# Four two-bank PSUM tiles split into one-bank tiles, and half of a transposition moved, in a graph attention kernel

## The chip, the cores and the metric

The kernel runs on one core of one Trainium2 chip. The metric is the device time of one execution in microseconds (us). All data are 32-bit floats.

## What is computed

The input x has 16 batches of 1024 nodes with 256 channels; `adj` is one 1024 x 1024 matrix shared by all batches. Two residual layers follow each other, each with a layer norm over the channels. The reference, cut to what matters:

```
# layer 0: x = layernorm(x + attention(x))
c_adj = mean over channels of x                       # one number a node
A     = 2 * | |sigmoid(c_adj[m] - c_adj[n]) - 0.5| - 0.5 |   # symmetrised
g     = relu((x^T @ (adj * A)) * para)                # 256 x 1024 a batch
q     = g^T, in 4 heads of 64
k, v  = split(x @ kv_w), in 4 heads of 64
out   = softmax(q k^T * scale) v

# layer 1: x = layernorm(x + 0.5 * (x + h))
h = relu(x @ w1_loop + adj @ (x @ w1_neigh) + b1)     # 128 channels
h = relu(h @ w2_loop + adj @ (h @ w2_neigh) + b2)     # 256 channels
```

In the second graph convolution the kernel multiplies `adj @ h` first (the product u) and applies `w2_neigh` after it.

## The kernel before

**Layout.** 1024 nodes are 8 tiles of 128 partitions (NT), 256 channels are 2 (NC), and a row of 1024 is 2 halves of 512 (NJ, FB), the size of one bank of PSUM. [...]The pool `psum` gives them out in two rings: `big_psum` has three tiles of two banks each, `bank_psum` has two tiles of one bank each. A new tile takes the place of the oldest of its ring, and the first instruction that writes it waits until the last reader of the old one is done.

**Order.** Instructions of each engine run in the order in which the code issues them (`manual_schedule`); there is no planner. One pass of the loop over b does the attention of batch b, the graph convolution of batch b - 1, and the preparation of batch b + 1. The attention has four units (a pair of heads and half of the queries each). For each unit:

- `scores(u)`: eight tiles s of scores on TensorE in the big ring (L377), eight exponentials on ScalarE (L380), and on VectorE the running sum of the eight results, acc (L384, L386), its transposition accB (L388) and its reduction den_part (L390). Ahead of the fourth tile, `halfway` puts in `add` of the unit before (den_ps in the bank ring, L409, read on VectorE by L413 to L415, then L417 to L420), and in unit 1 also `means` of the next batch (L206 in the bank ring, read by L213).
- `outputs(u)`: sixteen products with v, in the tile av of the bank ring (L397). VectorE transposes av into o (L401) after all of its work of `scores(u)`.
- Between the units stand the pieces of the graph convolution: `first` after unit 0, `second` after unit 1, `last` after unit 2. In the last batch only `first` stands there, and `second` and `last` come after the squares of the norm.

After unit 3 come the product g of the next batch (`step`, L345, with its weights wg from L331, L332 and L337), the blocked norm (`mean`, `squares`, `variance`, with two more tiles of the bank ring for its sums), and `keys` and `values` of the next batch. After the loop, `first`, `second` and `last` run once more for batch 15.

**Where the change is.** `values` makes v in two big tiles of four pieces of 256 columns each, and ScalarE empties a big tile in two copies. `first` makes t1 (L489, L492), then one big tile for h: the loop products of both halves (L497), then the products with the transposed adjacency for each half (L502), each half emptied by a ReLU into h1T (L504). `second` transposes h1T in one big tile (L514, L515), and makes u in another (L520, L522). `last` uses uT and h1T (L531, L532) and is read by VectorE (L534, L537). SBUF rows such as pr, acc, accB, t1, h1T, h1, uT and the loaded xB tiles share one ring of 15 (`row_tile`). SyncE's queue issues the DMAs: x and xB of the next batch, the spreading of the normed rows into x1, and the output.

Of the kernel before, what the change touches and what calls it, by code (L numbers as in the profile page):

```python
# [12 lines left out]
AF = mybir.ActivationFunctionType  # L13
# [5 lines left out]
def kernel(  # L19
# [31 lines left out]
    nc = tc.nc  # L51

    B, N, C = x.shape
    P = 128
    NT = N // P
# [4 lines left out]
    FB = 512  # L60
    NJ = N // FB
    TJ = FB // P
# [18 lines left out]
    def big_psum(name):  # L81
        return psum.tile([P, N], F32, tag="big", name=name, bufs=3)

    def bank_psum(name):
        return psum.tile([P, FB], F32, tag="bank", name=name, bufs=2)
# [6 lines left out]
    def row_tile(name):  # L92
        return work.tile([P, N], F32, tag="row", name=name, bufs=ROWS)

    def load_blocked(b, name):
        tiles = []
        for cc in range(NC):
            t = row_tile(f"xB_{name}_{cc}")
            for a in range(Q):
                c0 = cc * P + a * S  # L100
                nc.sync.dma_start(
                    out=t[a * S:(a + 1) * S, :].rearrange("k (bn r) -> k bn r", r=S),
                    in_=x[b, :, c0:c0 + S].rearrange("(bn k) r -> k bn r", k=S))
            tiles.append(t)
        return tiles
# [7 lines left out]
    w1l_sb = const.tile([P, NC, HID], F32, name="w1l_sb")  # L113
# [3 lines left out]
    b1_sb = const.tile([HID, 1], F32, name="b1_sb")  # L117
# [18 lines left out]
    ident = const.tile([P, P], F32, name="ident")  # L136
# [18 lines left out]
    adjT_sb = const.tile([P, NT, N], F32, name="adjT_sb")  # L155
# [38 lines left out]
    def prepare(blocked, name):  # L194

        xT = channel_major(blocked, f"xT_{name}")
        part = small.tile([P, NC, NB], F32, tag="part", name=f"part_{name}", bufs=2)
        for cc in range(NC):
            nc.vector.tensor_reduce(part[:, cc, :], blocked[cc].rearrange("p (bn r) -> p bn r", r=S), AX.X, ALU.add)
        return xT, part  # L200
# [90 lines left out]
    def keys(b, xT):  # L291
        kT = work.tile([P, NC, N], F32, tag="kT", name=f"kT_{b}")
        for kb in range(NC):
            pk = big_psum(f"k_ps_{b}_{kb}")
            for j in range(NJ):
                for cc in range(NC):
                    nc.tensor.matmul(pk[:, ts(j, FB)], kvw_sb[:, cc, ts(kb, P)], xT[:, cc, ts(j, FB)],  # L297
                                     start=(cc == 0), stop=(cc == NC - 1))
            nc.scalar.copy(kT[:, kb, :], pk)
        return kT  # L300

    def values(b, xT):
        v = work.tile([P, NT, C], F32, tag="v", name=f"v_{b}")
        per = N // C
        for g in range(NT // per):
            pv = big_psum(f"v_ps_{b}_{g}")
            for i in range(per):
                for cc in range(NC):
                    nc.tensor.matmul(pv[:, ts(i, C)], xT[:, cc, ts(g * per + i, P)], kvw_sb[:, cc, C:2 * C],  # L309
                                     start=(cc == 0), stop=(cc == NC - 1))  # L310
                if i % 2:
                    nc.scalar.copy(v[:, g * per + i - 1:g * per + i + 1, :],  # L312
                                   pv[:, (i - 1) * C:(i + 1) * C].rearrange("p (i c) -> p i c", c=C))
        return v

    class Queries:
# [161 lines left out]
    class GraphConv:  # L478
# [5 lines left out]
        def first(self):  # L484
            b, xT = self.b, self.xT
            p1 = big_psum(f"t1_ps_{b}")
            for t in range(NT):
                for cc in range(NC):
                    nc.tensor.matmul(p1[:, ts(t, HID)], xT[:, cc, ts(t, P)], w1n_sb[:, cc, :],  # L489
                                     start=(cc == 0), stop=(cc == NC - 1))  # L490
            t1 = row_tile(f"t1_{b}").rearrange("p (t f) -> p t f", f=HID)
            nc.scalar.copy(t1, p1.rearrange("p (t f) -> p t f", f=HID))  # L492

            ph = big_psum(f"h1_ps_{b}")
            for j in range(NJ):
                for cc in range(NC):
                    nc.tensor.matmul(ph[:, ts(j, FB)], w1l_sb[:, cc, :], xT[:, cc, ts(j, FB)],  # L497
                                     start=(cc == 0), stop=False)
            self.h1T = row_tile(f"h1T_{b}")
            for j in range(NJ):  # L500
                for mt in range(NT):
                    nc.tensor.matmul(ph[:, ts(j, FB)], t1[:, mt, :], adjT_sb[:, mt, ts(j, FB)],  # L502
                                     start=False, stop=(mt == NT - 1))
                nc.scalar.activation(self.h1T[:, ts(j, FB)], ph[:, ts(j, FB)], AF.Relu, bias=b1_sb)  # L504

        def second(self):

            b = self.b
            h1 = row_tile(f"h1_{b}")
            pt = big_psum(f"h1n_ps_{b}")  # L510
            for j in range(NJ):
                for i in range(TJ):
                    t = j * TJ + i
                    nc.tensor.transpose(pt[:, ts(t, P)], self.h1T[:, ts(t, P)], ident)  # L514
                nc.scalar.copy(h1[:, ts(j, FB)], pt[:, ts(j, FB)])  # L515
            pu = big_psum(f"u_ps_{b}")
            self.uT = row_tile(f"uT_{b}")
            for j in range(NJ):
                for mt in range(NT):
                    nc.tensor.matmul(pu[:, ts(j, FB)], h1[:, ts(mt, P)], adjT_sb[:, mt, ts(j, FB)],  # L520
                                     start=(mt == 0), stop=(mt == NT - 1))
                nc.scalar.copy(self.uT[:, ts(j, FB)], pu[:, ts(j, FB)])  # L522

        def last(self):
            b, x = self.b, self.x
# [22 lines left out]
    def run():  # L548
# [13 lines left out]
        for t in range(3):  # L562
            q.weigh(t)
        v = values(0, xT)
        for t in range(NT):
            if t + 3 < NT:
# [4 lines left out]
        for b in range(B):  # L571
# [20 lines left out]
            def halfway(u):  # L592
                att.add(u - 1)
                if u == 1 and more:
                    ready["mean"] = means(ready["part"], str(b + 1))

            between = [first, second, last] if more else [first]
            for u in range(len(UNITS)):
                if b == 0:
# [13 lines left out]
            if more:  # L613
# [26 lines left out]
                norm.scale()  # L640
                norm.spread()
                kT, v = keys(b + 1, xT), values(b + 1, xT)
            else:
                att.add(3)
                norm.mean()
                norm.squares()
                second()
                norm.variance()
                norm.scale()
# [28 lines left out]
    with tc.If(count < P):  # L678
        with tc.For_i(0, B, 1) as b:
            xb = load_x(b, "z")  # L680
            xT, part = prepare(load_blocked(b, "z"), "z")
            q = Queries("z", xb, *means(part, "z"))
            kT, v = keys("z", xT), values("z", xT)
            for t in range(NT):
                q.weigh(t)
                q.step(t)
            safe_attention("z", xb, q.end(), kT, v)
            layernorm(xb, "za")
            conv = GraphConv("z", xb, channel_major(blocked_of(xb, "z"), "x1T_z"))
            conv.first()  # L690
            conv.second()
            conv.last()
            conv.moments()
            conv.finish(out[b])
# [29 lines left out]
```

## Time and profile before

| | us |
|---|---|
| median of three runs | 2475.52 (2475.50 to 2475.76) |
| the profiled execution | 2474.71 |
| its span, first to last instruction | 2473.0 |
| mean granted TensorE clock | 0.99 of full speed |

| engine | busy us | share of the span |
|---|---|---|
| TensorE matmuls (PE) | 2343.9 | 95% |
| TensorE weight loads (PEld) | 1093.1 | 44% |
| VectorE (DVE) | 1540.1 | 62% |
| ScalarE (ACT) | 970.0 | 39% |
| GpSimd (POOL) | 128.6 | 5% |

A busy share is an average over stages that differ. A TensorE row shows an instruction from its start to the end of its latency, so rows of the same engine overlap and a busy time is not the time in which the engine could do no more. One matmul of the code is two instructions in the profile. Brackets behind a row give the idle time of the engine ahead of it and the instruction that ended it. The batches in the middle of the run are alike to a hundredth of a microsecond and follow each other every 150.15 us, so one of them stands for them all.

### The profile page before, as it was taken

How to read it: one execution, taken by the hardware profiler on the slowest of the kernel's cores; microseconds unless marked ns; L12 is line 12 of the kernel's file. 1: busy time of each engine (PE TensorE's matmuls, PEld its weight loads, DVE VectorE, ACT ScalarE, POOL GpSimd, SP SyncE). 2: the span in 40 equal slices, each digit the busy share in tenths (PEclk: the TensorE clock that was granted, in tenths of full speed). 3: DMA queues.
4: the chain of work that ended last, by engine and by line, in shares of the span. 5: the costliest groups of instructions: out<-in, count | busy, mean ns of one | idle time of the engine just before them, and what ended most of it. 6: DMA issues, size and time to landing. Idle time of an engine off the chain costs nothing.

```text
span 2473.0 us, 22370 instructions
## 1 busy us (share of the span) xinstructions
PE 2343.9 (95%) x8534; PEld 1093.1 (44%) x8534; DVE 1540.1 (62%) x2015; ACT 970.0 (39%) x1044; POOL 128.6 (5%) x45
## 2 busy tenths in 40 slices
PE   7899999999999999999999999999999999999976
PEld 4344444444444344444444444444443444444443
DVE  2865846748476484755758467484764847557553
ACT  3533524425343343524435244253433435244410
POOL 0000000100001010010100001000010100101000
PEclk9999999999999999999999999999999999999988
DMA  7422050320503113050230503205031140502001
GB/s 172 67 29 42 1 85 1 46 40 1 85 1 54 32 25 61 0 85 1 40 46 1 85 1 46 40 1 86 1 57 29 27 59 0 86 1 40 12 5 48
DMA packets 466674, 95.01 MB, mean 38 GB/s; under 512 B 431360, under 2 KB 465024, under 8 KB 466560
## 3 DMA queue, kind: packets, MB, share of 16 engines
q1 hardware_dynamic: 464864, 87.74, 23.2%
q10 hardware_dynamic: 1696, 5.77, 0.6%
q8 instruction: 69, 1.13, 0.2%
q14 instruction: 45, 0.37, 0.1%
HBM read 59.90 MB, written 16.78 MB: 31 GB/s over the span
## 4 chain that ended last, share of the span: by engine, by line
PE 77%; DVE 17%; ACT 4%; issue 1%; DMA 1%; POOL 0%; DVEq 0%; ACTq 0%; POOLq 0%
PE g_ps L345 18%; PE s L377 13%; PE av L397 12%; PE u_ps L520 9%; PE h_ps L502 9%; DVE acc L386 6%; PE v_ps L309 5%; PE k_ps L297 4%; PE t_ps L489 2%; PE h_ps L497 2%; DVE wg L337 2%; DVE z L534 1%; ACT pr L380 1%; DVE accB L388 1%; DVE acc L384 1%
## 5 line engine op out<-in xcount | busy, mean ns | idle before, releaser
L380 ACT ACTIVATE pr<-s 128x1024 f32<-128x1024 f32 x512 | 484.2, 1036 | 204.3 <-PE s L377 203.4
L377 PE MATMUL s<-qT,kT 64*128 64x512 f32 x2048 | 478.4, 607 | 18.4 <-DVE z L534 17.7
L386 DVE TENSOR_TENSOR acc<-acc,pr 128x1024 f32<-128x1024 f32 x384 | 470.1, 1224 | 35.3 <-DVE acc L386 0.5
L345 PE MATMUL g_ps<-wg,x 128*128 128x512 f32 x1024 | 456.0, 599 | 0.0
L397 PE MATMUL av<-pr,v 128*64 128x512 f32 x2048 | 453.6, 595 | 0.0
L384 DVE TENSOR_TENSOR acc<-pr,pr 128x1024 f32<-128x1024 f32 x64 | 78.1, 1221 | 517.2 <-ACT pr L380 517.2
L377 PEld LDWEIGHTS s<-qT,kT 64*128 64x128 f32 x2048 | 186.4, 187 | 256.2 <-issue 145.2
L345 PEld LDWEIGHTS g_ps<-wg,x 128*128 128x128 f32 x1024 | 190.6, 191 | 228.9 <-issue 209.5
L397 PEld LDWEIGHTS av<-pr,v 128*64 128x64 f32 x2048 | 141.3, 137 | 304.4 <-issue 266.8
L520 PE MATMUL u_ps<-adjT_sb,h 128*128 128x512 f32 x512 | 229.2, 601 | 10.9 <-ACT uT L522 10.9
L502 PE MATMUL h_ps<-adjT_sb,t 128*128 128x512 f32 x512 | 226.6, 595 | 12.4 <-ACT h1T L504 12.4
L337 DVE SCALAR_TENSOR_TENSOR wg<-wg,adj_sb 128x1024 f32<-128x1024 f32 x128 | 151.1, 1210 | 24.7 <-ACT wg L332 24.7
L502 PEld LDWEIGHTS h_ps<-adjT_sb,t 128*128 128x128 f32 x512 | 96.0, 190 | 139.7 <-issue 114.8
L520 PEld LDWEIGHTS u_ps<-adjT_sb,h 128*128 128x128 f32 x512 | 95.7, 192 | 133.0 <-issue 108.8
L331 ACT ACTIVATE wg<-c_row,c_col 128x1024 f32<-128x1024 f32 x128 | 146.6, 1146 | 14.6 <-DVE accB L388 12.7
L309 PE MATMUL v_ps<-kvw_sb,xT 128*128 128x256 f32 x512 | 123.4, 389 | 28.6 <-ACT v L312 27.8
L169 DVE STREAM_TRANSPOSE xT<-xB 128x1024 f32<-128x1024 f32 x30 | 37.2, 1242 | 161.8 <-DMA xB<-in_x_dram 161.8
L332 ACT ACTIVATE wg<-wg 128x1024 f32<-128x1024 f32 x128 | 135.4, 1058 | 4.2
L232 POOL TENSOR_TENSOR rstd_g<-rstd_g,neg_half 128x8 f32<-128x8 f32 x16 | 37.7, 2359 | 1902.5 <-DVE rstd_g L231 1902.5
L504 ACT ACTIVATE h1T<-h_ps,b_sb 128x512 f32<-128x512 f32 x32 | 22.0, 687 | 264.3 <-PE h_ps L502 264.3
L309 PEld LDWEIGHTS v_ps<-kvw_sb,xT 128*128 128x128 f32 x512 | 95.7, 192 | 60.1 <-ACT v L312 40.6
L297 PE MATMUL k_ps<-xT,kvw_sb 128*128 128x512 f32 x256 | 112.9, 594 | 0.0
(89 smaller groups left out, 1792.5 us busy)
## 6 DMA issues: line engine op xcount, KB each, us to landing
x<-in_x_dram SPq DMA_DIRECT2D x16, 1024.0 KB, 6.3
xB_a<-in_x_dram SPq DMA_DIRECT2D x128, 128.0 KB, 4.6
x<-xB_a SPq DMA_DIRECT2D x512, 32.0 KB, 2.0
out_dram<-x SPq DMA_DIRECT2D x16, 1024.0 KB, 5.0
xB<-in_x_dram SPq DMA_DIRECT2D x120, 128.0 KB, 4.5
adj_sb<-in_adj_dram ACTq DMA_DIRECT2D x8, 512.0 KB, 6.7
adjB<-in_adj_dram SPq DMA_DIRECT2D x32, 128.0 KB, 4.1
para_sb<-in_L_gnn_para_dram ACTq DMA_DIRECT2D x1, 1024.0 KB, 10.1
```

What stands on the lines that cost most here:

```text
L297: nc.tensor.matmul(pk[:, ts(j, FB)], kvw_sb[:, cc, ts(kb, P)], xT[:, cc, ts(j, FB)], start=(cc == 0), stop=(cc == NC - 1))
L309: nc.tensor.matmul(pv[:, ts(i, C)], xT[:, cc, ts(g * per + i, P)], kvw_sb[:, cc, C:2 * C], start=(cc == 0), stop=(cc == NC - 1))
L331: nc.scalar.activation(wg, self.c_row, AF.Abs, bias=self.c_col[:, t:t + 1], scale=-1.0)
L332: nc.scalar.activation(wg, wg, AF.Tanh, scale=-0.5)
L337: nc.vector.scalar_tensor_tensor(wg, wg, 1.0, adj_sb[:, t, :], op0=ALU.add, op1=ALU.mult)
L345: nc.tensor.matmul(self.pg[cb][:, ts(j, FB)], self.xb[:, t, ts(cb, P)], wg[:, ts(j, FB)], start=(t == 0), stop=(t == NT - 1))
L377: nc.tensor.matmul(ps[:, ts(s, FB)], self.kT[rows, pair, ts(mt, P)], self.qT[rows, pair, ts(j, FB)], start=True, stop=True)
L380: nc.scalar.activation(pr, ps, AF.Exp)
L386: nc.vector.tensor_add(acc, acc, pr)
L397: nc.tensor.matmul(pav[s * HD:(s + 1) * HD, :], self.v[:, mt, pair * P + s * HD:pair * P + (s + 1) * HD], self.pr[mt][:, ts(s, FB)], start ...
L502: nc.tensor.matmul(ph[:, ts(j, FB)], t1[:, mt, :], adjT_sb[:, mt, ts(j, FB)], start=False, stop=(mt == NT - 1))
L520: nc.tensor.matmul(pu[:, ts(j, FB)], h1[:, ts(mt, P)], adjT_sb[:, mt, ts(j, FB)], start=(mt == 0), stop=(mt == NT - 1))
```

## The change

v, h, the transposed h1 and u get one tile of the bank ring for each half (v: for each pair of pieces) instead of two-bank tiles of the big ring. In `first`, the loop products of a half now stand directly ahead of the adjacency products of that half. The transposition of h1T is a function of its own, `turn`; its first half is done at the end of `first`, its second half at the beginning of `second`. The row for h1 is taken in `first`. The number of matmuls, of transpositions and of copies is the same.

```diff
     def values(b, xT):
         v = work.tile([P, NT, C], F32, tag="v", name=f"v_{b}")
-        per = N // C
+        per = FB // C
         for g in range(NT // per):
-            pv = big_psum(f"v_ps_{b}_{g}")
+            pv = bank_psum(f"v_ps_{b}_{g}")
             for i in range(per):
                 for cc in range(NC):
                     nc.tensor.matmul(pv[:, ts(i, C)], xT[:, cc, ts(g * per + i, P)], kvw_sb[:, cc, C:2 * C],
                                      start=(cc == 0), stop=(cc == NC - 1))
-                if i % 2:
-                    nc.scalar.copy(v[:, g * per + i - 1:g * per + i + 1, :],
-                                   pv[:, (i - 1) * C:(i + 1) * C].rearrange("p (i c) -> p i c", c=C))
+            nc.scalar.copy(v[:, g * per:(g + 1) * per, :], pv.rearrange("p (i c) -> p i c", c=C))
...
-            ph = big_psum(f"h1_ps_{b}")
+            self.h1T = row_tile(f"h1T_{b}")
+            self.h1 = row_tile(f"h1_{b}")
             for j in range(NJ):
+                ph = bank_psum(f"h1_ps_{b}_{j}")
                 for cc in range(NC):
-                    nc.tensor.matmul(ph[:, ts(j, FB)], w1l_sb[:, cc, :], xT[:, cc, ts(j, FB)],
-                                     start=(cc == 0), stop=False)
-            self.h1T = row_tile(f"h1T_{b}")
+                    nc.tensor.matmul(ph, w1l_sb[:, cc, :], xT[:, cc, ts(j, FB)], start=(cc == 0), stop=False)
+                for mt in range(NT):
+                    nc.tensor.matmul(ph, t1[:, mt, :], adjT_sb[:, mt, ts(j, FB)], start=False, stop=(mt == NT - 1))
+                nc.scalar.activation(self.h1T[:, ts(j, FB)], ph, AF.Relu, bias=b1_sb)
+            self.turn(0)
+
+        def turn(self, j):
+
+            pt = bank_psum(f"h1n_ps_{self.b}_{j}")
+            for i in range(TJ):
+                nc.tensor.transpose(pt[:, ts(i, P)], self.h1T[:, ts(j * TJ + i, P)], ident)
+            nc.scalar.copy(self.h1[:, ts(j, FB)], pt)
+
+        def second(self):
+
+            self.turn(1)
+            self.uT = row_tile(f"uT_{self.b}")
             for j in range(NJ):
-                for mt in range(NT):
-                    nc.tensor.matmul(ph[:, ts(j, FB)], t1[:, mt, :], adjT_sb[:, mt, ts(j, FB)],
-                                     start=False, stop=(mt == NT - 1))
-                nc.scalar.activation(self.h1T[:, ts(j, FB)], ph[:, ts(j, FB)], AF.Relu, bias=b1_sb)
-
-        def second(self):
-
...
-            pu = big_psum(f"u_ps_{b}")
-            self.uT = row_tile(f"uT_{b}")
-            for j in range(NJ):
-                for mt in range(NT):
-                    nc.tensor.matmul(pu[:, ts(j, FB)], h1[:, ts(mt, P)], adjT_sb[:, mt, ts(j, FB)],
-                                     start=(mt == 0), stop=(mt == NT - 1))
-                nc.scalar.copy(self.uT[:, ts(j, FB)], pu[:, ts(j, FB)])
+                self.neighbours(j)
+
+        def neighbours(self, j):
+            pu = bank_psum(f"u_ps_{self.b}_{j}")
+            for mt in range(NT):
+                nc.tensor.matmul(pu, self.h1[:, ts(mt, P)], adjT_sb[:, mt, ts(j, FB)],
+                                 start=(mt == 0), stop=(mt == NT - 1))
+            nc.scalar.copy(self.uT[:, ts(j, FB)], pu)
```

## The prediction

> **What bounds the kernel now.** I read the page first, then the waits, then the order of time of one batch, engine by engine, then the granted clock over short stretches.
>
> From the page, the engines (busy us, share of the span, instructions):
>
> ```profile
> PE 2343.9 (95%) x8534; PEld 1093.1 (44%) x8534; DVE 1540.1 (62%) x2015; ACT 970.0 (39%) x1044; POOL 128.6 (5%) x45
> ```
>
> TensorE sets the time, but a busy bar holds the matmul's latency (0.59 us) and not its spacing: 16 instructions of 512 columns come every 0.429 us. So I count starts, and look for TensorE's stalls. From the list of waits (us in total, times, longest):
>
> ```profile
> PE v_ps L309 <- ACT v L312: 27.8, 32, 6.8
> PE h1n_ps L514 <- ACT h L515: 13.7, 16, 3.4
> PE h_ps L502 <- ACT h1T L504: 12.4, 16, 0.8
> PE u_ps L520 <- ACT uT L522: 10.9, 16, 0.7
> ```
>
> In each, the second half of a two-bank tile waits until ScalarE has emptied the first half. These are what the change takes away. Now unit 1 of a steady batch (they repeat every 150.15 us), TensorE and then VectorE (start, length, engine, line, and in brackets the idle time before):
>
> ```profile
> 671.17 2.85 PE L377 MATMUL s<-qT,kT 64*128 64x512 f32 x12
> ...
> 674.74 4.56 PE L377 MATMUL s<-qT,kT 64*128 64x512 f32 x20
> 679.23 7.09 PE L397 MATMUL av<-pr,v 128*64 128x512 f32 x32
> 686.25 0.66 PE L514 MATMUL h1n_ps<-ident,h1T 128*128 128x128 f32 x4
> 687.58 0.65 PE L514 MATMUL h1n_ps<-ident,h1T 128*128 128x128 f32 x4 [0.68 <-ACT h L515]
> 688.07 7.03 PE L520 MATMUL u_ps<-adjT_sb,h 128*128 128x512 f32 x16
> 695.78 7.13 PE L520 MATMUL u_ps<-adjT_sb,h 128*128 128x512 f32 x16 [0.68 <-ACT uT L522]
> 702.84 2.85 PE L377 MATMUL s<-qT,kT 64*128 64x512 f32 x12
> ```
>
> ```profile
> 674.33 1.23 DVE L384 TENSOR_TENSOR acc<-pr,pr 128x1024 f32<-128x1024 f32 x1 [7.38 <-ACT pr L380]
> ...
> 681.27 6.53 DVE L386 TENSOR_TENSOR acc<-acc,pr 128x1024 f32<-128x1024 f32 x5
> 687.84 1.25 DVE L388 STREAM_TRANSPOSE accB<-acc 128x1024 f32<-128x1024 f32 x1
> 689.12 1.22 DVE L390 TENSOR_REDUCE den_part<-accB 128x32 f32<-128x1024 f32 x1
> 690.25 0.71 DVE L401 STREAM_TRANSPOSE o<-av 128x512 f32<-128x512 f32 x1
> ```
>
> The reader is to see that the attention output av is complete at 686.3, yet VectorE, which runs without a gap from 674.33, reads it out of its bank only at 690.25 to 690.96. Nobody minds now: the next user of that bank comes a unit later.
>
> Last, what a TensorE gap of this size costs. In batch 0 it waited 2.40 us for VectorE at 121.38. The stretches just before and after (PEclk, the granted clock, stands ahead of the last two numbers), and the matmuls that followed:
>
> ```profile
> 118.20:121.50 3.30, 0.90 (x5) 0.12 (x2) 3.23 (x4) 1.96 (x3) 0.00 (x0) 1.00 0.10 16
> 121.60:125.00 3.40, 3.40 (x10) 1.61 (x11) 3.40 (x4) 1.02 (x1) 0.00 (x0) 0.50 0.92 134
> ```
>
> ```profile
> 121.76 6.16 PE L377 MATMUL s<-qT,kT 64*128 64x512 f32 x20
> ```
>
> Twenty matmuls took 6.16 us instead of the 4.56 of the unit above: 1.60 us lost to half a clock for 3.41 us.
>
> **What the Trainium skill says.** "TensorE: Matmul & The Clock Gate" (What's actually happening) puts the clock at half after an idle window of about 3.4 us, the windows running free. The trace agrees, and is stricter: 2.4 us idle in one window were enough at 121, 1.78 us at 104.28 were not, and at 2377.9 to 2381.1 a window still 2.55 us busy stayed at half until 2384.6. The same page (PE-mode transpose) says that transposes don't count as busy in this; no run here shows it alone, but it would lengthen the gap below. "PSUM — Partial Sum Buffer" (PSUM bank collisions) asks for semaphores by bank, since two engines may not touch one bank at once; so nobody may write av's bank before VectorE has read it, and the waits above fall on different banks, so they come from the tile and not from the bank.
>
> **The change, part by part.** Times are for one steady batch. Every matmul in the code is two instructions in the profile; their number doesn't change, nor does any ScalarE, VectorE or DMA instruction.
>
> *v.* Before: 626.22 to the next unit at 635.11, 8.89 us, of which 32 instructions of 0.2145 us are 6.86. In one-bank tiles a piece is 1.72 us, and its copy of 0.58 us is over before its bank comes round again. With 0.1 us for the change of shape, 6.96: gain 1.93. Fifteen times 29.0. In the first v, the copies stand on ScalarE behind six activations until 28.90. Two pieces instead of one run ahead, and the last two follow at 29.5, partly at half clock: g would start at some 34.7 instead of 37.38, gain 2.7.
>
> *h.* From 652.87 to 671.17, 18.30 us. Forty instructions of 0.429 are 17.15; the stall goes, the four transposes of turn(0) come in (0.5), two changes of shape 0.2: 17.85, gain 0.45. Fifteen times 6.8. Covers: t1 is needed after four loop instructions (654.59) instead of eight; its copy ends at 654.08, so 0.5 us is left. The extra copy on ScalarE runs between h1T and the first exponential and ends about 0.9 us after the scores start, when that exponential starts at 1.18; without that cover it would cost up to 0.58.
>
> *h1n and u.* Half of the transposes are gone from here, and both stalls. But the tiles now rotate through the two "bank" buffers: den, mean, av of unit 1, h1n, u, u. In the built program h1n takes the bank of mean (read by 679.8) and **the first u takes the bank of av**; it waits for VectorE's o (L401), the last instruction of that run. Relative to the start of the scores (671.17): VectorE starts at 3.16, 16.6 us of its work follow, o ends at 19.79; a semaphore there to TensorE costs 0.07 (sum after o at 2370.78), so u starts at 19.86 instead of 16.90. TensorE would be ready at 15.08 + 0.5 = 15.6: it stands idle for about 4.1 us. Behind the waiting matmul are all 32 of u and the scores of unit 2; VectorE and ScalarE then have nothing else to do. From u on 13.92 us, so unit 2 starts at 33.78 instead of 31.67: loss 2.11, in the 14 batches 1 to 14: 29.5.
>
> *Batch 15 and the end.* There the second stage stands behind the squares, its u needs only the bank of sum (free at once), and the wait of 3.39 us at 2378.55 lies under the first four u matmuls: gain some 6.6. The closing stage saves its three stalls: 2.1.
>
> *Queues.* SP: one of the loaded xB tiles now takes the slot of accB, free at 649.99; SP itself is busy issuing x until 650.37. Nothing. Those tiles are reduced at 666.95, and TensorE asks at 674.19, under 2.4 us sooner after the change. POOL and the ACT queue: unmoved.
>
> *Clock.* A gap of 4.1 us (4.6 with the transposes) nearly always leaves over 2.2 us in one window of 3.41, so half clock follows, over u, which is all TensorE: one window costs 1.7 us. Where the gap straddles two windows, part of the half window lies in the gap (down to 0.8), but then it may stay for a second one (2.5). Fourteen times 0.9 to 2.0: 13 to 28 us. I take 1.7 each: 24.
>
> *Sum.* 29.0 + 2.7 + 6.8 + 6.6 + 2.1 - 29.5 = 17.7 gained; minus 24: 6.3 lost. The profiled execution took 2474.71 us (span 2473.0), 0.8 under the median of 2475.52: 2481.0 for it, **2482** for the median.
>
> **The rivals.**
> 1. *Forecast: stalls removed, a longer one put in, and half a clock behind it.* For it, the order of the banks and the row at 690.25. With 13 to 28 us for the clock: 2471 to 2486. Chance 0.72.
> 2. *The gap doesn't slow the clock* (the other side). The place is u behind av, 14 times; the price is zero instead of 1.7 us. It decides from 1.26 us per stall (17.7 / 14): below that the kernel is faster. For it: 1.78 us at 104.28 did nothing, and the windows could fall so that each gap is halved. Against it: all the gaps over 2.3 us in the trace were followed by half clock. 2475.5 - 17.7 = 2458, to 2464 with a few hits. Chance 0.17.
> 3. *u doesn't wait*, so the change does all that it says: h1n and u take 14.4 instead of 16.59 us, gain 30.4 in place of the loss of 29.5: 2475.5 - 77.6 = 2398. Against it: VectorE's run of 16.6 us has no slack. Chance 0.05.
> 4. *Half clock for two whole windows each time*, as at 2371 to 2384: 14 x 2.6 = 36 us: 2494. Chance 0.06.
>
> **How the numbers follow.** 0.2% is 5 us, about what a measurement of this kernel can tell from no change. Case 1 is slower by more where the clock costs over 22.7 us (two thirds of it, 0.48), and within 0.2% below that (0.24). Slower: 0.48 + 0.06 = 0.54; same 0.24; faster 0.22. Both signs hold much of it: case 1 alone is 2471 to 2486. The range 2456 to 2491 leaves out case 3, the low edge of 2 and most of 4.
>
> **What would show it.** Right: in the waits, a row of u on VectorE's o, 14 times some 4 us; no waits of v, h, u on their own copies; half-clock stretches after 671 in most batches; twelve or more. Wrong: u starting within 17 us of the unit's scores (3), or a clock of 1.00 in the steady batches with the u rows still waiting (2). If o ends much before 19.8, my reading of VectorE's run fails.

## The result, and the profile after

The changed kernel took 2485.15 us (median of four runs, 2483.23 to 2486.05), the kernel before 2475.51 on the same chip (four runs, 2474.18 to 2475.76). The ratio is 1.0039, 95% interval 1.0022 to 1.0056: slower by some 0.4%. The forecast was 2482 in a range of 2456 to 2491. In the profiled execution the span went from 2473.0 to 2483.8 us, 10.8 longer, and the mean granted clock of TensorE from 0.990 to 0.977.

The engines, from the page of the changed kernel (busy us, share of the span, instructions):

```profile
PE 2356.8 (95%) x8534; PEld 1111.9 (45%) x8534; DVE 1540.0 (62%) x2015; ACT 968.4 (39%) x1044; POOL 128.5 (5%) x45
```

No instruction count moved, and VectorE and ScalarE are as busy as they were. TensorE is busy for 12.9 us more with the same 8534 instructions, so some of them ran slower. The row of u among the costliest groups (busy, mean ns of one, idle just before and what ended it) names them. First as it was before, then as it is now:

```profile
L520 PE MATMUL u_ps<-adjT_sb,h 128*128 128x512 f32 x512 | 229.2, 601 | 10.9 <-ACT uT L522 10.9
L520 PE MATMUL u_ps<-adjT_sb,h 128*128 128x512 f32 x512 | 256.0, 664 | 57.8 <-DVE o L399 57.8
```

The list of TensorE's waits in the changed kernel (us in total, times, longest) shows where the stalls went:

```profile
PE u_ps L520 <- DVE o L399: 57.8, 14, 4.5
PE s L375 <- DVE z L534: 17.7, 14, 1.3
...
PE v_ps L309 <- ACT v L311: 5.0, 1, 5.0
...
PE h1n_ps L507 <- ACT h1T L500: 0.3, 1, 0.3
```

All four waits on own copies are gone but for the very first v; the 0.3 us of h1n at the end are a wait for its input h1T. In their place u now waits for VectorE's o (line 399 here, 401 before), 14 times, 57.8 us. The z row is as it was before; experiment 6 comes back to it. One steady batch of the changed kernel in order of time, TensorE (start, length, engine, line, and in brackets the idle time before):

```profile
629.26 7.07 PE L309 MATMUL v_ps<-kvw_sb,xT 128*128 128x256 f32 x32
636.26 7.14 PE L375 MATMUL s<-qT,kT 64*128 64x512 f32 x32
...
654.02 1.88 PE L497 MATMUL h_ps<-x1T,w1l_sb 128*128 128x512 f32 x4
...
671.19 0.60 PE L507 MATMUL h1n_ps<-ident,h1T 128*128 128x128 f32 x4
671.72 2.85 PE L375 MATMUL s<-qT,kT 64*128 64x512 f32 x12
...
679.78 7.09 PE L395 MATMUL av<-pr,v 128*64 128x512 f32 x32
686.80 0.66 PE L507 MATMUL h1n_ps<-ident,h1T 128*128 128x128 f32 x4
691.55 16.71 PE L520 MATMUL u_ps<-adjT_sb,h 128*128 128x512 f32 x32 [4.10 <-DVE o L399]
708.19 2.85 PE L375 MATMUL s<-qT,kT 64*128 64x512 f32 x12
```

and VectorE in the same batch:

```profile
688.38 1.25 DVE L386 STREAM_TRANSPOSE accB<-acc 128x1024 f32<-128x1024 f32 x1
689.66 1.22 DVE L388 TENSOR_REDUCE den_part<-accB 128x32 f32<-128x1024 f32 x1
690.79 0.71 DVE L399 STREAM_TRANSPOSE o<-av 128x512 f32<-128x512 f32 x1
```

The thirty-two instructions of v now run through in 7.00 us. The product h with four transposes behind it takes 654.02 to 671.72. Then av is complete at 686.87, VectorE reads it from 690.79 to 691.50, and u starts at 691.55. This u took 16.71 us, against 13.90 in experiment 1, where nothing waits. Stretches of two batches (us; length; then busy time and instructions of TensorE, its weight loads, VectorE, ScalarE and GpSimd; granted clock; DMA share; GB/s) say why:

```profile
690.30:693.50 3.20, 1.95 (x3) 0.91 (x4) 1.20 (x2) 0.00 (x0) 0.00 (x0) 0.50 0.00 0
693.70:696.90 3.20, 3.20 (x5) 1.14 (x5) 0.00 (x0) 0.00 (x0) 0.00 (x0) 0.50 0.00 0
697.10:704.00 6.90, 6.90 (x17) 3.07 (x17) 0.00 (x0) 0.59 (x1) 0.00 (x0) 1.00 0.00 0
840.50:843.70 3.20, 0.00 (x0) 0.00 (x0) 3.13 (x4) 0.04 (x1) 0.00 (x0) 1.00 0.00 0
843.90:847.10 3.20, 3.08 (x4) 1.51 (x5) 0.06 (x1) 0.00 (x0) 0.00 (x0) 0.50 0.00 0
847.40:852.00 4.60, 4.60 (x12) 2.10 (x11) 0.00 (x0) 0.00 (x0) 0.00 (x0) 1.00 0.02 4
```

In the records of this trace the clock changes only on a grid of 3.413 us; one step of it is called a window here. In the batch at 840 the gap fills one window, the next window is at half, and then the clock is whole again. In the batch at 690 the half window still contains the tail of the gap (1.95 us busy of 3.20), and the window after it stays at half too. The first kind costs u 15.57 - 13.90 = 1.67 us, the second 16.71 - 13.90 = 2.81. The 14 steady batches are seven of each in turn: 7 x (1.67 + 2.81) = 31 us. The turn is no accident: the longer half-clock stretches start at 386.43, 690.21 and 994.00 us, so two batches together take 303.79 us, which is 89 windows, and each gap meets the grid at the same place as two batches earlier.

The account of the 10.8 us: a batch took 150.16 us before and takes 151.33 and 152.46 in turn now (with the kind of gap). From the start of batch 1's v to that of batch 15's, which holds all 14 waits, it was 2102.2 us (175.76 to 2277.92) and is 2126.6 (174.13 to 2300.68): 24.4 lost. What lies outside this stretch gained 13.6.

### The profile page after: what moved, and what is told of

Same layout as the page of the kernel before. It is cut to its first block, busy times and chain, and to the rows that moved or that the text cites. A ratio compares the mean times of both kernels' runs of the same rounds, so it can differ in the third digit from the quotient of the medians.

```text
span 2483.8 us, 22397 instructions
## 1 busy us (share of the span) xinstructions
PE 2356.8 (95%) x8534; PEld 1111.9 (45%) x8534; DVE 1540.0 (62%) x2015; ACT 968.4 (39%) x1044; POOL 128.5 (5%) x45
## 4 chain that ended last, share of the span: by engine, by line
PE 69%; DVE 26%; ACT 2%; issue 2%; DMA 1%; POOL 0%; DVEq 0%; ACTq 0%; POOLq 0%
PE g_ps L343 18%; PE u_ps L520 10%; DVE acc L384 10%; PE s L375 9%; PE h_ps L499 9%; PE av L395 8%; PE v_ps L309 4%; PE k_ps L297 4%; PE t_ps L487 2%; PE h_ps L497 2%; DVE wg L335 2%; ACT pr L378 2%; DVE accB L386 2%; DVE acc L382 2%; DVE den_part L388 2%
## 5 line engine op out<-in xcount | busy, mean ns | idle before, releaser
L375 PE MATMUL s<-qT,kT 64*128 64x512 f32 x2048 | 478.6, 607 | 18.4 <-DVE z L534 17.7
L520 PE MATMUL u_ps<-adjT_sb,h 128*128 128x512 f32 x512 | 256.0, 664 | 57.8 <-DVE o L399 57.8
L520 PEld LDWEIGHTS u_ps<-adjT_sb,h 128*128 128x128 f32 x512 | 108.7, 216 | 195.5 <-issue 134.3
L522 ACT COPY uT<-u_ps 128x512 f32<-128x512 f32 x32 | 18.7, 585 | 292.0 <-PE u_ps L520 292.0
L309 PE MATMUL v_ps<-kvw_sb,xT 128*128 128x256 f32 x512 | 116.0, 385 | 5.0 <-ACT v L311 5.0
```

The source lines that it names most:

```text
L375: nc.tensor.matmul(ps[:, ts(s, FB)], self.kT[rows, pair, ts(mt, P)], self.qT[rows, pair, ts(j, FB)], start=True, stop=True)
L520: nc.tensor.matmul(pu, self.h1[:, ts(mt, P)], adjT_sb[:, mt, ts(j, FB)], start=(mt == 0), stop=(mt == NT - 1))
```

## The experiments

Ratios are to the kernel before, on the same chip. The theory to be tested: **the bank ring hands u a bank that VectorE empties last of its run (some 58 us), and the clock adds some 31 us to that; the splitting itself gains some 80 us.** The rivals: that u would wait for something else once the bank is free, that the clock's loss has another origin than the gap, that the gains of the splitting are not worth what the sum says.

### 1. Another bank for the second half of h1n (e1_h1n_half_big)

```diff
-            pt = bank_psum(f"h1n_ps_{self.b}_{j}")
+            pt = (big_psum if j else bank_psum)(f"h1n_ps_{self.b}_{j}")[:, 0:FB]
```

Half of a two-bank tile serves for the second transposition, so one user fewer stands in the ring of two bank buffers: the first u gets the bank of mean, the second the bank of av, 6.9 us later.

> The changed kernel, but the second half of the transposed h1 goes to a tile of the big ring. Then the first u takes mean's bank, which is free, and only the second u takes the bank of av, 6.9 us later, when VectorE has read it. Bank theory: the 14 waits of about 4.1 us before u go, and with them the half clock behind them (1.69 or 2.82 us a batch): 14 x (4.28 + 2.26) = 92 us under the changed kernel, near 2394 us, clock 1.00 in the steady batches. Rival (TensorE must wait for VectorE's run for another reason, data or another bank): the wait moves to another instruction and the time stays within 10 us of 2485.

Measured: 2393.91 us, ratio 0.9676 (0.966 to 0.9692), clock 0.991. The order of time of TensorE in this kernel:

```profile
666.99 0.66 PE L507 MATMUL h1n_ps<-ident,h1T 128*128 128x128 f32 x4
667.48 13.90 PE L520 MATMUL u_ps<-adjT_sb,h 128*128 128x512 f32 x32
681.31 2.85 PE L375 MATMUL s<-qT,kT 64*128 64x512 f32 x12
```

u follows the transposes with no gap, starts 15.56 us behind the unit's first scores (651.92) instead of 19.83, and runs in 13.90 us. From the changed kernel to this one the ratio falls by 0.0363, 90 us; the wait (57.8) and the clock (31) are 89. One tile's place in the ring is the whole loss, and the rest of the change is worth 3.2% of the time.

### 2. VectorE reads av earlier (e4_o_first)

In the changed kernel the transposition of acc and its reduction are moved behind that of o. The bank that u gets is the same; VectorE's order differs.

```diff
-            accB = row_tile(f"accB_{b}_{u}")
-            nc.vector.transpose(accB, acc)
...
             nc.vector.transpose(self.o, pav)
+            self.sums_of(u)
```

(The new function sums_of holds the removed lines and the reduction that stood behind them.)

> The changed kernel with VectorE's order turned in every unit: av is transposed into o ahead of accB and den_part instead of behind them. The bank stays shared, but it is free 2.45 us sooner: u starts at 17.4 us behind the scores' start, with 1.7 us idle. Bank theory: 14 x 2.45 = 34 us for the wait, and 31.6 us for the clock if 1.7 us is too short to slow it: near 2420 us; if the clock still falls in part, up to 2445. Rival (a wait for VectorE's whole run): no change, 2485.

Measured: 2414.84 us, ratio 0.9765 (0.9749 to 0.9781), clock 0.991. The waits of TensorE in this kernel:

```profile
PE u_ps L525 <- DVE o L403: 22.1, 14, 1.6
PE den_ps L412 <- DVE den_part L392: 15.9, 21, 3.2
```

The wait for o stays but falls from 4.1 to 1.6 us, about the 2.5 us of the two instructions that were moved, and 1.6 us never halved the clock in a steady batch. So the wait is for o on VectorE and its length is VectorE's run. What is later for it, den_part, costs little: that row was 10.4 us in the changed kernel. It came out 5 us better than expected. The z wait is gone here too: the same scores now wait for ScalarE's exponential instead (3.7 us, 14 times 0.27). I read this from the built program as a score tile that got another of the three two-bank slots; the traces do not name slots, so they do not show it.

### 3. The first transposition back in its old place (e5_turn0_late, e9_turn0_late_big)

e5 takes experiment 1 and moves the first half of h1n behind av again, to see what that half of the change is worth:

```diff
-            self.turn(0)
...
         def second(self):
+            self.turn(0)
             self.turn(1)
```

> The first experiment (second half of the transposed h1 in a big tile, 2394 us) with the first half of the transposition put back into the second stage. If the early turn is worth little beside the banks: u waits for one copy, some 0.3 us a batch longer, 14 x 0.3 = 4 us: near 2398. Rival (the early turn carries the second stage's gain, because the copy of 0.58 us and its latency stand in the path again): 14 x 0.85 to 1.3 us, 2406 to 2413.

Measured: 2484.23 us, ratio 1.0042 (1.0025 to 1.0059), clock 0.977: neither expectation held. The order of time in this kernel shows the changed kernel's gap over again:

```profile
684.04 1.09 PE L506 MATMUL h1n_ps<-ident,h1T 128*128 128x128 f32 x8
688.90 16.79 PE L520 MATMUL u_ps<-adjT_sb,h 128*128 128x512 f32 x32 [3.77 <-DVE o L399]
```

What both overlooked is that moving turn(0) also moves its bank tile in the ring. It now comes after den, mean and av, takes the bank of mean, and hands u the bank of av once more. That reading was then tested with both halves of h1n in two-bank tiles (e9), which leaves mean's bank to u:

```diff
-            pt = (big_psum if j else bank_psum)(f"h1n_ps_{self.b}_{j}")[:, 0:FB]
+            pt = big_psum(f"h1n_ps_{self.b}_{j}")[:, 0:FB]
```

> The fifth experiment with both halves of the transposed h1 in tiles of the big ring, so that the first u takes mean's bank again and not that of av; the first half of the transposition stays in the second stage. It differs from the first experiment (2394 us) only in the place of those four transposes. Bank theory: the fifth experiment was slow because its first half took mean's bank and left av's to u; here u waits only for one copy, some 0.3 us: 2394 to 2400 us. Rival (the late transposition itself costs the time): near 2484.

Measured: 2404.89 us, ratio 0.972 (0.9704 to 0.9737). 79 us came back from one line, as the ring theory says. It ended 5 us above the upper end expected, because u now waits briefly for the copy of the second half:

```profile
669.86 14.00 PE L520 MATMUL u_ps<-adjT_sb,h 128*128 128x512 f32 x32 [0.24 <-ACT h L507]
```

A batch takes 145.89 us instead of 145.39 in experiment 1. So the early transposition is worth 0.5 us a batch, 7 us over the steady batches and 11 in the whole (by the ratios, 0.0044).

### 4. The gap filled with work (e2_fill4, e6_fill2)

Four or two matmuls whose result isn't used are put into the gap of the changed kernel, into a two-bank tile. TensorE still can't start u before o, but it is not idle meanwhile. This separates the wait from the clock.

```diff
             self.turn(1)
+            if fill:
+                pf = big_psum(f"fill_ps_{self.b}")
+                for k in range(fill):
+                    nc.tensor.matmul(pf[:, 0:FB], self.h1T[:, ts(k, P)], adjT_sb[:, k, 0:FB], start=True, stop=True)
```

> The changed kernel with four needless matmuls (8 instructions, 3.43 us) into an unused big tile ahead of u in batches 1 to 14; their result is not used. The wait for the bank stays and u starts at the same point, 19.86 us behind the scores' start; only TensorE's idle time falls to some 0.7 us. Clock theory: no half clock in the steady batches, 31.6 us less than the changed kernel: near 2454 us, some 22 us under the kernel before. Rival (the clock follows from something else than the gap, or its loss lies beside other work): 2480 to 2487 us.

Measured: 2456.13 us, ratio 0.993 (0.9914 to 0.9947), clock 0.992, a batch 149.80 us. The order of time in this kernel:

```profile
681.11 3.60 PE L516 MATMUL fill_ps<-adjT_sb,h1T 128*128 128x512 f32 x8
685.39 14.00 PE L524 MATMUL u_ps<-adjT_sb,h 128*128 128x512 f32 x32 [0.68 <-DVE o L399]
```

Needless work made the kernel faster than the one before, by 0.7%, and against the changed kernel by 0.0109 of the time, 27 us. u starts no earlier; the clock alone is what came back, close to the 31 us above. So this is also what the change would have brought if the gap had not slowed the clock: 0.993 of the time before is 2458, the low end of the prediction's second case (2458 to 2464).

With two matmuls 2.4 us of gap are left.

> The changed kernel with two needless matmuls (1.7 us) ahead of u in batches 1 to 14 instead of four; some 2.4 us of TensorE's gap are left, as long as the one at 121 us of the kernel before, which was followed by half clock. If a gap of 2.4 us slows the clock only where it lies nearly whole in one window of 3.41 us: 3 to 6 of the 14 batches, 1.7 us each, 2461 to 2467 us. Rivals: every time (2480 us), or never (2456 us, as with four).

Measured: 2461.08 us, ratio 0.9949 (0.9932 to 0.9965). Half clock followed in four of the 14 steady batches, and the gap's length did not decide which. Two batches in this kernel's order of time, and the stretches around the first:

```profile
686.87 14.00 PE L524 MATMUL u_ps<-adjT_sb,h 128*128 128x512 f32 x32 [2.39 <-DVE o L399]
...
836.62 15.65 PE L524 MATMUL u_ps<-adjT_sb,h 128*128 128x512 f32 x32 [2.39 <-DVE o L399]
```

```profile
833.20:836.50 3.30, 1.03 (x3) 0.19 (x1) 3.23 (x4) 0.00 (x0) 0.00 (x0) 1.00 0.00 0
836.70:840.00 3.30, 3.30 (x4) 1.43 (x5) 0.00 (x0) 0.00 (x0) 0.00 (x0) 0.50 0.02 5
```

The same 2.39 us cost nothing at 686 and 1.65 us at 836, where they lay in one window. Splitting each gap over the windows (the grid laid through the places where the records change the clock), the four that were followed by half clock had 2.12, 2.33, 2.38 and 2.11 us in one window; of the other ten none had more than 1.97.

### 5. v alone, and all but v (e3_v_alone, e7_without_v)

e3 is the kernel before with the change in v alone; e7 is the changed kernel with v as it was before. The edit is the same, once made and once taken back:

```diff
-        per = N // C
+        per = FB // C
...
-            pv = big_psum(f"v_ps_{b}_{g}")
+            pv = bank_psum(f"v_ps_{b}_{g}")
```

> The kernel before with the split of v alone. By my sum 15 x 1.93 + 2.7 = 31.7 us gained: near 2444 us. Rival (the freed time is taken back by a later wait in the units, or ScalarE's copies delay the first exponentials): 2460 us or more.

Measured: 2441.93 us, ratio 0.9874 (0.9857 to 0.989).

> The changed kernel with v as before: the split of h, of the transposed h1 and of u alone. If the parts add up: 31.6 us over the changed kernel, near 2516, or 41 us slower than the kernel before. The half clock goes by how the gaps lie in the windows, so 14 x 1.0 to 2.8 us for it instead of 31.6: 2499 to 2525. Rival (v's gain is what made the gap, through a rotation moved by four tiles): near 2475.

Measured: 2514.45 us, ratio 1.0167 (1.015 to 1.0184). The waits of TensorE in e7 hold both the old row and the new one:

```profile
PE u_ps L522 <- DVE o L401: 57.8, 14, 4.4
PE v_ps L309 <- ACT v L312: 27.8, 32, 6.8
```

v is worth 31.6 us alone, and taking it from the changed kernel costs 0.0128 of the time, 31.7. The prediction's sum was 29.0 + 2.7 = 31.7. The two ways agree well within the noise, so v's gain simply adds to the rest.

### 6. Can the z wait go too? (e8_last_first, e10_big_o_first)

With u free, TensorE's longest row in experiment 1 is the wait of the scores for z, 17.7 us. e8 takes experiment 1 and issues the last part of the convolution, with its z, ahead of the next batch's weighing:

```diff
+                if u < len(between):
+                    between[u]()
                 if u == 2 and more:
...
-                if u < len(between):
-                    between[u]()
```

> The first experiment, and in unit 2 the last stage of the graph convolution is issued ahead of the weights of the next batch, so that VectorE reads z before its three products wg. The wait of the scores of unit 3 for z (14 times 1.26 us) should go: 14 x 1.3 = 18 us, near 2376. Rival (the scores then wait for the exponentials, or the first g for wg): 2388 us or more.

Measured: 2413.73 us, ratio 0.9757 (0.9741 to 0.9773): a miss, 20 us slower than experiment 1. The waits of TensorE in this kernel begin with

```profile
PE den_ps L407 <- DVE den_part L388: 39.1, 18, 5.0
```

The z row is gone, and the row of den_part grew from 10.6 us to 39.1. VectorE has a backlog, and z was only the place where it showed. Worse, in the new order VectorE waits for the tiles of the last part before it comes to the weighing, 0.27 and 0.97 us, and everything behind gets later by that. In a steady batch TensorE now stands idle ahead of den_ps:

```profile
727.71 0.62 PE L407 MATMUL den_ps<-den_part,fold 128*128 128x32 f32 x2 [1.98 <-DVE den_part L388]
```

The two rows account for 28.5 - 17.7 = 11 of the 20 us. The clock, 0.987 instead of 0.991, accounts for the rest: in six of the 14 steady batches this gap lay whole in one window and half clock followed, and these batches take 147.69 us instead of 146.00, together 10 us.

e10 takes experiment 1 and puts o first, as in experiment 2 (the same edit).

> The first experiment with VectorE's order of the fourth: av is transposed into o ahead of accB and den_part. No wait for av is left in the first experiment, so the turn can only bring what the fourth showed beside it: the built program gives the slot of z to a later tile of the scores (up to 14 x 1.26 us gained), and den_part comes 0.7 us later for den_ps (14 x 0.4 us lost). Near 2385 us. Rival (VectorE's backlog decides, as in the eighth): 2394 or more.

Measured: 2390.94 us, ratio 0.9664 (0.9648 to 0.968). That lies between the two expectations, and its interval overlaps that of experiment 1: the two can't be told apart. Its batch takes 144.91 us against 145.39; the z wait is gone, but den_part waits 21 times, 18.8 us. Experiments 1 and 10 beat both kernels, by some 3.3% over the one before.

## Why the prediction was right, and where its size was off

**What bounds, and the stalls removed.** The four rows disappeared as said. v: 8.89 - 7.00 = 1.89 us a batch (1.93 predicted), shown by e3 and e7. h with its transposes: 18.30 - 17.70 = 0.60 (0.45 predicted). The two covers held: t1 and the extra copy on ScalarE appear in no wait of the steady batches.

**The bank of av.** The step was the decisive one, and held to hundredths: u starts 691.55 - 671.72 = 19.83 us behind the scores (19.86 predicted), idle 4.1. Shown by experiments 1 and 2, and, against my own expectation, by e5. Without the clock the stage loses 19.83 + 13.83 - 31.67 = 1.99 us (2.11), with 13.83 for u from experiment 1. That u doesn't wait, the third case, is what experiment 1 built: 2394 measured, 2398 forecast for it.

**The clock: the term that was mis-sized.** It was taken at 24 us, 1.7 for each of 14, within bounds of 13 to 28. Half clock followed in all 14 (twelve or more were forecast), but it cost 31, above the term's own upper bound. The working said that a half window with idle time in it "may stay for a second one (2.5)" and then took the price of a single window for all; seven of the 14 stayed, at 2.81 each. That the time still fell inside the first case (2471 to 2486) is luck: with 31 us for the clock and the other terms as predicted, the sum gives 2475.5 - 17.7 + 31 = 2489. (The half clock at 2371 to 2384 that the fourth case names as its model lasted four windows, 13.65 us, and not two.) Whether a gap causes the half clock at all was a forecast from few gaps in the trace of before; experiment 4 shows it.

**Start, batch 15, closing stage.** Predicted 2.7 + 6.6 + 2.1 = 11.4 us. Measured from the two traces: g of batch 0 starts at 35.75 instead of 37.38, gain 1.6; from the last av to the end of u in batch 15 31.20 instead of 36.62, gain 5.4; from the first t to the last product of the closing stage 43.47 instead of 47.59, gain 4.1. Together 11.1; the 2.5 us that are left of the 13.6 are the v of batch 15 and the h of its pass (1.89 + 0.60), which come after the 14 waits. The closing stage gained more than its three stalls since 30 instructions of t took 3.62 us instead of 5.24: before, they fell into a half-clock window. That is where the windows happened to lie, and no merit of the change.

**The sum.** Without the clock it came to 31 - 10.8 = 20.2 us gained (17.7 predicted), with it 10.8 lost in the span (6.3 predicted). Two errors of opposite sign, 7 and 2.5 us, left 4.5 us in the span and 3 in the median.

## What to carry to other kernels

When a tile is split to take away a wait on its own copy, list the order in which its pool's ring is then walked: the wait may only have moved to the previous user of the bank, and moving an instruction that owns a tile shifts every later one in the ring. Cost a gap of TensorE twice, once for its length and once for what it does to the clock, and for the second ask how it falls in the windows. A row of waits that names an instruction at the end of a busy engine's run names the run, and reordering that run only renames the row.

## What the runs showed of the hardware

With two matmuls in the gap (e6) the idle time of a gap inside one 3.41 us window decided: 2.11 us were enough for half a clock in the next, and 1.97 us were not. With the last part first (e8) a gap of 1.97 to 1.98 us was enough all six times that it lay whole in one window, so the bound is near 2 us and not the idle time alone. "TensorE: Matmul & The Clock Gate" (Why this matters for your kernels) advises no gaps above about 3 us; here 2.4 us were too many when they lay in one window, and harmless when they straddled two.

The way back is stricter than expected: a window at half clock that was busy for only 1.95 of 3.20 us was followed by a second at half. One that was busy for 3.08 of 3.20 was followed by the whole clock. In the steady batches of e5 the bound shows more closely: a half window busy for 2.80 of its 3.41 us (from 1749.30) was followed by the whole clock, one busy for 2.78 (from 991.54) by a second half.

The prediction lengthened the gap by the transposes ahead of it, which were not to count as busy. The traces show that here they count at least in part: in e7 the window from 1156.55 us held 1.85 us of idle time and 0.59 of transposes alone, 2.44 together and more than the 2.11 of idle time that were enough in e6, and the whole clock followed.
